# Four attention heads' logits issued together, with four PSUM banks for logits and two for everything else

## The chip, the cores and the metric

The kernel runs on one core of one Trainium2 chip. The metric is device time in microseconds (us) of that core. TensorE is PE below, its weight loads are PEld, VectorE is DVE, ScalarE is ACT and GpSimd is POOL.

## The reference, cut to what matters

The input is 4 images of 128 channels and 64x64 pixels. Everything is fp32.

```python
y  = layernorm_over_channels(x);  y = y + depthwise_3x3(y)
xw = y cut into windows of 16x16 pixels
q, k, v = xw @ Wq, Wk, Wv                   # 2 branches, 4 heads of 32
logits  = q . k over a 5x5 neighbourhood, scaled
o  = softmax(logits) . v
x  = x + (o @ Wo, the branches combined)
t  = tokens of x
t  = t + causal_linear_attention(layernorm(t))
t  = t + recurrence(batchnorm(layernorm(t) @ W))    # sigmoid(wx + y @ V.T), step by step
```

The change concerns the window attention. It is 16 bands of 16 image rows, each of four windows, and behind each band runs the causal linear attention of the band before. The recurrence at the end is the same in both kernels.

## The kernel before

The kernel takes PSUM in banks of 512 fp32 columns. Three pools share eight of them (3 + 2 + 3):

```python
ps_s = main.enter_context(tc.tile_pool(name="ps_s", bufs=3, space=PSUM))   # logits
ps_o = main.enter_context(tc.tile_pool(name="ps_o", bufs=1, space=PSUM))   # ops, dps: one bank each
ps_m = main.enter_context(tc.tile_pool(name="ps_m", bufs=3, space=PSUM))   # everything else

def bank(pool=ps_m, tag="bank"):
    return pool.tile([P, 512], F32, tag=tag, name=tag)
```

"Everything else" is q, k, v of a window, the normalisations, and all of the linear attention. A normalisation keeps one bank (`vps`) for its variances and takes a further one for each chunk:

```python
def variance(vps, at, src, n, keep=None):      # keep is given for the band's own normalisation
    cps = bank()
    nc.tensor.matmul(cps[:, : n * P], center, src, start=True, stop=True)         # L161
    if keep is not None:
        nc.vector.tensor_copy(keep, cps[:, : n * P])                               # L163
    sq = p2.tile(...)
    nc.scalar.activation(sq[:, : n * P], cps[:, : n * P], AF.Square)               # L165
    for j in range(n):
        nc.tensor.matmul(vps[:, at + j : at + j + 1], sq[:, j * P : ...], mean_col, ...)  # L167
# [...] then rstd on DVE (L156); spread() makes diag from it on POOL (L145) and multiplies on PE (L149)
```

The logits of one head use one row group of 32 rows of the PE array and get a bank of their own. The weighted sums end in a reciprocal on DVE and an addition on POOL, which only feeds a check of the final result:

```python
def logits(w, heads):
    sps = {h: bank(ps_s, "sps") for h in heads}
    # [...] mask, L266
    for br, n in pieces:
        for h in heads:
            nc.tensor.matmul(sps[h][:, cols], w["k"][rows, ...], w["q"][rows, cols], ...)  # L271
    # [...] exp on ACT, L280

def weighted(w):
    # [...] L293, L301, L304 into ops and dps
    nc.vector.reciprocal(rden, dps)                              # L306
    nc.gpsimd.tensor_tensor(rtot, rtot, rden, ALU.add)           # L307
    nc.vector.tensor_tensor(oT, ops, rden, ALU.mult)             # L309
    nc.vector.tensor_tensor(rmin, rmin, rden, ALU.min)           # L310

# the loop over windows; the framework's scheduler orders each engine's instructions from this
if now:  logits(now, (0, 1))
if done: weighted(done)              # of the window before
next(behind, None)                   # a piece of the linear attention
if now:  logits(now, (2, 3))
next(behind, None)
# [...] output of the window before, normalisation of the next band (in the second window),
#       q, k, v of the next window, two more pieces of linear attention
```

## Time and profile before

| | before |
|---|---|
| median of 2 runs | 1768.87 us (1767.15 to 1770.59) |
| span and granted clock of the profiled run | 1750.5 us, 0.886 |
| PE, DVE, ACT, POOL busy | 89%, 62%, 31%, 22% |
| one steady band, windows A, B, C, D | 16.6, 21.2, 18.0, 41.0 us |

L149 has two forms, one for the linear attention (128x512) and one for the next band's normalisation (128x384). The columns of the view of groups are: line, engine and operation, output and inputs, shapes, count; then busy us and mean ns of one; then the us that the engine stood idle just before, and for what.

```profile
L167 PE MATMUL bank<-mean_col,sq 128*128 128x1 f32 x800 | 122.9, 275 | 28.9 <-ACT sq L165 28.5
...
L244 PE MATMUL bank<-wvT,y 128*128 128x256 f32 x384 | 94.2, 382 | 0.0
L307 POOL TENSOR_TENSOR rtot<-rtot,rden 128x512 f32<-128x512 f32 x64 | 81.2, 1268 | 418.8 <-DVE rden L306 398.1 <-DVE rstd L156 20.7
L149 PE MATMUL bank<-diag,ones 128*128 128x512 f32 x128 | 76.4, 682 | 15.5 <-POOL diag L145 15.4
...
L149 PE MATMUL bank<-diag,ln_g 128*128 128x384 f32 x96 | 67.8, 852 | 33.2 <-POOL diag L145 33.2
```

PE waits 28.9 us for the normalisation's squares (L167), not at all for v (L244), and little for the diag of the linear attention (the first form of L149). The second form, before the next band, waits 33.2 us.

### The profile page before, as it was taken

The page shows a single profiled execution, that of the slowest core. Times are in us where ns is not written, and L with a number is a line of the kernel's source. Part 1 is how long each engine was busy: PE and PEld are TensorE (multiplying, and loading weights), DVE is VectorE, ACT ScalarE, POOL GpSimd, SP SyncE. Part 2 cuts the span into 40 slices and gives each one's busy share as a digit, 9 for nine tenths or more (in the row PEclk, how much of TensorE's full clock was granted, in tenths as well). Part 3 has the DMA queues.
Part 4 walks back from the last instruction along what each step waited for, and adds up shares of the span by engine and source line. Part 5 has one row for each costly group of instructions (what it writes and reads, how often), then busy time and mean ns, then how long its engine had stood idle before and what let it go on. Part 6 is the DMA issues. An engine that isn't in the chain of part 4 may idle for free. (4 is left out here: it accounts for less than half of the span.)

```text
span 1750.5 us, 27470 instructions
## 1 busy us (share of the span) xinstructions
PE 1561.3 (89%) x11294; PEld 1048.6 (60%) x11294; DVE 1083.5 (62%) x2028; ACT 540.0 (31%) x924; POOL 383.2 (22%) x683
## 2 busy tenths in 40 slices
PE   5899999899998999899998999899998999976475
PEld 3566666576666666675766666665766666644232
DVE  3666656665666766575665766575656666644298
ACT  1332323333232333332232333332232333321142
POOL 1113121311213131211212131211212131211044
PEclk8888979897889999897889999897889999887596
DMA  1000000000000000000000000000000000000422
GB/s 53 1 15 1 27 1 12 15 1 26 1 27 1 27 1 14 13 7 21 1 27 1 27 1 22 6 7 20 1 27 1 27 1 13 1 13 0 204 85 110
DMA packets 13528, 37.61 MB, mean 21 GB/s; under 512 B 3409, under 2 KB 4690, under 8 KB 12882
## 3 DMA queue, kind: packets, MB, share of 16 engines
q1 hardware_dynamic: 11664, 30.88, 5.0%
q10 hardware_dynamic: 1730, 4.89, 0.7%
q8 instruction: 91, 1.49, 0.4%
q14 instruction: 43, 0.35, 0.1%
HBM read 18.98 MB, written 16.78 MB: 20 GB/s over the span
## 5 line engine op out<-in xcount | busy, mean ns | idle before, releaser
L271 PEld LDWEIGHTS sps<-q_sb,k_sb 32*128 32x128 f32 x3072 | 260.0, 192 | 93.9 <-issue 77.3
L271 PE MATMUL sps<-q_sb,k_sb 32*128 32x96 f32 (+1 forms) x3072 | 294.0, 285 | 0.0
L306 DVE RECIPROCAL rden<-dps 128x512 f32<-128x512 f32 x64 | 214.9, 3357 | 86.0 <-PE dps L304 85.0
L225 DVE SCALAR_TENSOR_TENSOR y<-ypad,cpe_w,y 128x256 f32<-128x256 f32 x512 | 244.2, 479 | 11.0
L280 ACT ACTIVATE es<-sps 128x512 f32<-128x512 f32 x256 | 141.7, 595 | 322.5 <-PE sps L271 322.2
L145 POOL TENSOR_SCALAR diag<-ident,rstd 128x128 f32<-128x128 f32 x400 | 146.9, 387 | 417.4 <-DVE rstd L156 276.2
L307 POOL TENSOR_TENSOR rtot<-rtot,rden 128x512 f32<-128x512 f32 x64 | 81.2, 1268 | 418.8 <-DVE rden L306 398.1
L167 PEld LDWEIGHTS bank<-mean_col,sq 128*128 128x128 f32 x800 | 114.5, 220 | 72.0 <-ACT sq L165 69.4
L167 PE MATMUL bank<-mean_col,sq 128*128 128x1 f32 x800 | 122.9, 275 | 28.9 <-ACT sq L165 28.5
L304 PE MATMUL dps<-es,ones 128*32 128x512 f32 x512 | 134.5, 666 | 0.0
L238 ACT COPY k_sb<-bank 128x512 f32<-128x512 f32 x64 | 37.5, 585 | 298.0 <-PE bank L234 298.0
L165 ACT ACTIVATE sq<-bank 128x512 f32<-128x512 f32 (+1 forms) x112 | 61.7, 551 | 200.5 <-DVE xc L163 104.9
L362 POOL TENSOR_TENSOR f<-f,low 128x512 f32<-128x512 f32 x64 | 81.5, 1275 | 186.1 <-ACT low L361 185.6
L149 PE MATMUL bank<-diag,ln_g 128*128 128x384 f32 x96 | 67.8, 852 | 33.2 <-POOL diag L145 33.2
L244 PE MATMUL bank<-wvT,y 128*128 128x256 f32 x384 | 94.2, 382 | 0.0
L149 PE MATMUL bank<-diag,ones 128*128 128x512 f32 x128 | 76.4, 682 | 15.5 <-POOL diag L145 15.4
L233 PE MATMUL bank<-y,wqT 128*128 128x256 f32 x256 | 82.3, 425 | 8.3 <-DVE y L225 8.3
L293 PE MATMUL ops<-es,v_sb 128*32 128x96 f32 (+1 forms) x3072 | 87.6, 257 | 0.0
L266 PE MATMUL sps<-mask_q,mask_k 32*128 32x512 bf16 x256 | 70.4, 398 | 19.2 <-ACT es L280 12.4
L236 DVE COPY q_sb<-bank 128x512 f32<-128x512 f32 x64 | 44.2, 691 | 69.8 <-PE bank L233 69.8
L361 ACT ACTIVATE low<-low 128x512 f32<-128x512 f32 x64 | 40.3, 631 | 138.3 <-DVE low L358 138.3
L244 PEld LDWEIGHTS bank<-wvT,y 128*128 128x128 f32 x384 | 73.7, 192 | 10.3
(129 smaller groups left out, 2415.7 us busy)
## 6 DMA issues: line engine op xcount, KB each, us to landing
wxd<-wxs SPq DMA_DIRECT2D x32, 256.0 KB, 2.0
out<-ot SPq DMA_DIRECT2D x16, 512.0 KB, 2.6
x_t<-in_x SPq DMA_DIRECT2D x8, 576.0 KB, 4.0
x_t<-in_x SPq DMA_DIRECT2D x8, 544.0 KB, 4.0
wx<-wxd SPq DMA_DIRECT2D x2, 2048.0 KB, 17.5
wx<-wxd ACTq DMA_DIRECT2D x2, 2048.0 KB, 13.0
x_t<-in_x SPq DMA_DIRECT2D x8, 32.0 KB, 3.8
awT<-in_awT ACTq DMA_DIRECT2D x1, 192.0 KB, 3.5
```

The lines of the kernel that those rows point to most:

```text
L145: nc.gpsimd.tensor_scalar(diag[:, j * P : (j + 1) * P], ident, rstd[j], 1.0, ALU.mult, ALU.mult)
L149: nc.tensor.matmul(bc[:, : n * P], rows, diag[:, : n * P], start=True, stop=True)
L167: nc.tensor.matmul(vps[:, at + j : at + j + 1], sq[:, j * P : (j + 1) * P], mean_col, start=True, stop=True,)
L225: nc.vector.scalar_tensor_tensor(y2v, src, cpe_w[:, tap : tap + 1], y2v, ALU.mult, ALU.add)
L233: nc.tensor.matmul(qps[:, cols], wqT[:, br * P : (br + 1) * P], y2, start=True, stop=True)
L244: nc.tensor.matmul(vps[:, c0 : c0 + 256], y2[:, k0 : k0 + P], wvT, start=True, stop=True)
L271: nc.tensor.matmul(sps[h][:, cols], w["k"][rows, k0 : k0 + P], w["q"][rows, cols], start=False, stop=(br, n) == pieces[-1],)
L280: nc.scalar.activation(es, sps[h], AF.Exp, scale=scale)
L293: nc.tensor.matmul(ops[rows, cols], w["v"][:, n, c0 : c0 + HD], w["es"][h][:, cols], start=(br, n) == pieces[0], stop=(br, n) == pieces[-1],)
L304: nc.tensor.matmul(dps[rows], ones[:, :HD], w["es"][h], start=False, stop=True)
L306: nc.vector.reciprocal(rden, dps)
L362: nc.gpsimd.tensor_tensor(f, f, low, ALU.add)
```

## The change

The intent: four heads sit in four row groups, which can run beside each other. Two heads at a time use half of the array. Issuing all four needs four banks for logits, and the fourth is taken from "everything else".

```diff
-    ps_s = main.enter_context(tc.tile_pool(name="ps_s", bufs=3, space=PSUM))
+    ps_s = main.enter_context(tc.tile_pool(name="ps_s", bufs=4, space=PSUM))
     ps_o = main.enter_context(tc.tile_pool(name="ps_o", bufs=1, space=PSUM))
-    ps_m = main.enter_context(tc.tile_pool(name="ps_m", bufs=3, space=PSUM))
+    ps_m = main.enter_context(tc.tile_pool(name="ps_m", bufs=2, space=PSUM))
@@
         if now:
-            logits(now, (0, 1))
+            logits(now, (0, 1, 2, 3))
         if done:
             weighted(done)
         next(behind, None)
-        if now:
-            logits(now, (2, 3))
         next(behind, None)
```

## The prediction

> **What bounds the kernel now.** I began with busy shares on the profile page, then cut one steady band of image rows (16 such bands make the attention stage) into its four windows, and then read the instruction timeline inside them.
>
> ```profile
> PE 1561.3 (89%) x11294; PEld 1048.6 (60%) x11294; DVE 1083.5 (62%) x2028; ACT 540.0 (31%) x924; POOL 383.2 (22%) x683
> ...
> L271 PE MATMUL sps<-q_sb,k_sb 32*128 32x96 f32 (+1 forms) x3072 | 294.0, 285 | 0.0
> L306 DVE RECIPROCAL rden<-dps 128x512 f32<-128x512 f32 x64 | 214.9, 3357 | 86.0 <-PE dps L304 85.0
> ```
>
> TensorE (PE) leads with 89%, VectorE (DVE) has 62%, and the logits (L271) are PE's largest group. The stretches, one window each, are: time, then busy us per engine, then the granted PE clock.
>
> ```profile
> core 0: us, PE busy (x) PEld busy (x) DVE busy (x) ACT busy (x) POOL busy (x), PEclk, DMA share, GB/s
> 451.25:467.86 16.61, 16.61 (x110) 13.13 (x109) 12.05 (x34) 6.14 (x10) 3.95 (x10) 1.00 0.01 1
> 467.86:489.03 21.17, 21.00 (x193) 15.38 (x191) 14.33 (x34) 6.34 (x11) 2.56 (x3) 1.00 0.01 2
> 489.03:507.07 18.04, 16.67 (x138) 9.79 (x138) 12.66 (x18) 6.56 (x12) 4.39 (x9) 0.95 0.08 30
> 507.07:548.10 41.03, 36.47 (x260) 24.03 (x259) 22.59 (x32) 12.62 (x20) 11.18 (x21) 0.83 0.06 15
> ```
>
> I call them A, B, C, D; together 96.85 us. In A and B PE has no idle time, so PE issue sets the pace. In D PE sits idle 4.6 us although all its other work is done: that is the next band's normalisation, where one chain of single instructions runs alone:
>
> ```profile
> 534.66 0.81 PE L161 MATMUL bank<-x_t,center 128*128 128x384 f32 x2
> ...
> 536.08 0.55 DVE L163 COPY xc<-bank 128x384 f32<-128x384 f32 x1
> ...
> 536.72 0.49 ACT L165 ACTIVATE sq<-bank 128x384 f32<-128x384 f32 x1 [3.03 <-DVE xc L163]
> ...
> 537.26 0.83 PE L167 MATMUL bank<-mean_col,sq 128*128 128x1 f32 x6 [1.47 <-ACT sq L165]
> ...
> 537.95 1.54 PE L161 MATMUL bank<-x_t,center 128*128 128x384 f32 x4
> 538.88 1.20 DVE L163 COPY xc<-bank 128x384 f32<-128x384 f32 x2 [1.06 <-PE bank L161]
> ```
>
> The last L161 row holds two of the three chunks at once (x4: two fp32 passes each): chunks two and three use two banks at the same time. Last, what a head's logits cost alone and beside another head:
>
> ```profile
> 105.20 1.58 PE L271 MATMUL sps<-q_sb,k_sb 32*128 32x96 f32 x24
> ...
> 126.87 1.57 PE L271 MATMUL sps<-q_sb,k_sb 32*128 32x96 f32 x12
> ```
>
> The first row is 24 passes of two heads that alternate, the second 12 passes of one head alone, both at full clock: the same time. So the row groups run beside each other, and a stretch of logits costs what its longest row group costs: in the second the single passes start 0.112 us apart on the mean of the trace's records, so a matmul of two passes costs 0.224 us.
>
> **What the Trainium skill says.** "TensorE: Matmul & The Clock Gate", Part 3 (packing small matmuls), says that matmuls in different row groups overlap, and gives 3.07x for four row tiles. The rows above show 2x for two; no row of this kernel has four heads at once, though L293 keeps four column tiles going (48 passes in about 1.09 us). "TensorEngine Tiling (Array Packing)", Gotcha 1, says that row tiling raises PSUM pressure because row tiles need different banks: that is the trade made here. "PSUM — Partial Sum Buffer", on bank collisions, has two engines' accesses to one bank put in order; in the trace L165 on ScalarE (ACT) waits for L163 on DVE each time (48 waits, 104.9 us), though both only read. The clock-gate page's Part 1 ties the clock to PE activity; here D, with its idle PE, has 0.83 granted and A and B have 1.00.
>
> **The change part by part**, per band; I compared the built order of each engine before and after.
>
> *Logits.* Cut the order into uninterrupted runs of L271 and take from each the count of its longest row group. Before, a band has 19 runs with 61 matmuls in the longest groups: 61 x 0.224 = 13.7 us. The L271 time in such a run not covered by the matmul before it sums to 257 us over the trace, 16.1 a band, so each run costs (16.1 - 13.7) / 19 = 0.12 us beside. After: 21 runs, 31 matmuls, 6.9 + 2.6 = 9.5 us. Gain 6.5 us, if four groups scale as two do.
>
> *Causal-attention loops* (L405, L409, L411, in A and B). With three banks the next numerator starts while the last is being read. With two, L405 waits for DVE's state add and L411 for the yt multiply; the built order shows both waits. A step on DVE is rd 0.16, state 0.28, reciprocal 0.16, yt 0.34 with one or two tap multiplies of 0.47 between. Laid beside 0.65 us of matmuls and shorter logits, I get some 0.2 us idle at each of six steps: loss 1.2 us.
>
> *Normalisation* (D). The running variance holds one bank, so two banks leave one for the chunks: L161, copy, square, L167, three times in a row. A chunk takes about 0.65 + 0.55 + 0.6 + 0.55 = 2.4 us; the two that ran together before took 0.8 less than two such chains, and the built order puts nothing between: loss 1.5 us. Also, DVE's order after has the second softmax reciprocal (3.36 us) just before the first L163. Before, that reciprocal came earlier, and L163 started 0.6 us after L161 ended. Adding 3.36 us behind the aT multiply, the residual add and the multiplies gives 3 us from L161's end to the copy: loss 2.4 us.
>
> *Window C.* The weighted sums now sit in a clump, so the reciprocal of one runs when C's q copy and the rstd reciprocal want DVE, and the rtot add (1.27 us) now stands before the four diag instructions (1.41 us) on POOL. PE's L149 then starts about 6.4 us after the first L233, against 492.54 - 489.03 = 3.5 before; some 1 us of that is work of its own, so loss 2.3 us. In D the L149 before the linear attention has no logits left to hide its diag behind: loss 1.1 us.
>
> Sum: 6.5 - 1.2 - 3.9 - 2.3 - 1.1 = -2.0 us a band. With 15 bands behind the first, that is 30 us lost, or 1799 us. I take 1796, a little less, because the last band has no next normalisation to wait for.
>
> **The rivals.** (1) PE is the bound, and the whole logits gain lands: 16 x 6.5 = 104 us, 1665 us. For it: PE 89%. Against: the built order shows the waits above on exactly the banks that were taken away. (2) Half of it lands, because the losses in C and D hide behind weighted sums that I placed wrongly: 1768.87 - 50 = 1720 us. (3) Four row groups don't scale, with a quarter more per pass: 9.5 becomes some 11.2 us, another 27 us lost, 1825 us. (4) The longer idle time of PE in D draws a lower clock into C and A; window D already pays about 4 us for half-clock stretches, and as much again in each band would be 64 us, 1850 us.
>
> **Range and chances.** The net is a difference of 6.5 and 8.5, each good to perhaps 2 us, so about 3 us a band, 48 us: 1745 to 1850. Under 1733 everything in C and D would have to be free: 0.12. Over 1804 needs 0.3 us a band more than I have: 0.36. The rest, 0.52, is within 2%.
>
> **What would show it.** L271's rows should hold four heads, with its busy time down by a third or so. PE's idle time before L405 or L411 should be there for DVE, where the page of before has 4.1 us for L405. L167's wait for sq (28.5 us of PE idle time) should at least double. The normalisation from the first L161 to the first L233, 13.4 us before, should be near 17. If L405 doesn't wait and that stays at 13 us, the banks weren't needed and I am wrong towards faster; if A to D all grow with the clock down, towards slower.

## More of the kernel before

The timeline of POOL around window C of the prediction shows why the first form waits so little. The addition L307 has run long before rstd comes, and diag starts at once:

```profile
484.10 1.27 POOL L307 TENSOR_TENSOR rtot<-rtot,rden 128x512 f32<-128x512 f32 x1 [5.20 <-DVE rden L306]
491.08 3.12 POOL L145 TENSOR_SCALAR diag<-ident,rstd 128x128 f32<-128x128 f32 x8 [5.71 <-DVE rstd L156]
```

## The result, and the profile after

The changed kernel took 1885.37 us (1884.81 to 1885.93, two runs). The ratio to before is 1.066, with a 95% interval of 1.061 to 1.071. Ratios here are the mean time of one kernel's runs over that of the other's in the same rounds, so not quite the ratio of the quoted medians. Executions over 1.5% slower than the fastest of the same kernel are left out of the means. The prediction was 1796 us with a range to 1850: right that the change doesn't pay, wrong on how much it costs.

The page of the changed kernel, the lines for the engines, the logits and the softmax reciprocal:

```profile
PE 1564.7 (83%) x11294; PEld 936.6 (50%) x11294; DVE 1083.7 (58%) x2028; ACT 537.5 (29%) x924; POOL 385.1 (20%) x683
...
L306 DVE RECIPROCAL rden<-dps 128x512 f32<-128x512 f32 x64 | 214.6, 3353 | 35.4 <-PE dps L304 35.3
...
L271 PE MATMUL sps<-q_sb,k_sb 32*128 32x96 f32 (+1 forms) x3072 | 195.7, 304 | 0.0
```

The logits' busy time fell from 294.0 to 195.7 us, yet PE's total rose by 3 us. So nearly as much was added in other matmuls, which are the same in number: they ran slower, or with less beside them (busy times of lines that run beside each other overlap, so this is no exact balance). The span and the mean granted clock of the two profiled runs, before and then after:

```profile
core 0: 1750.5 us, clock 0.886
```
```profile
core 0: 1882.7 us, clock 0.862
```

One band of the changed kernel in its four windows A to D, cut at the same instruction as in the prediction (the first L233 of each window); columns as there:

```profile
core 0: us, PE busy (x) PEld busy (x) DVE busy (x) ACT busy (x) POOL busy (x), PEclk, DMA share, GB/s
697.73:716.94 19.21, 19.11 (x142) 12.62 (x141) 12.55 (x34) 6.16 (x10) 4.46 (x9) 0.97 0.01 1
716.94:740.38 23.44, 22.51 (x217) 14.77 (x215) 14.38 (x33) 6.95 (x12) 1.53 (x3) 1.00 0.01 1
740.38:755.52 15.14, 11.24 (x78) 6.06 (x76) 12.13 (x19) 3.64 (x6) 4.53 (x9) 1.00 0.05 18
755.52:803.17 47.65, 38.57 (x264) 22.09 (x265) 22.47 (x31) 14.75 (x25) 11.20 (x21) 0.76 0.06 19
```

D grew by 6.6 us, and its clock fell from 0.83 to 0.76. A and B grew by 2.6 and 2.3 us, and C shrank by 2.9, but some matmuls only changed places: C has 78 left of 138. The mean over the steady bands is about 98 us before (single bands take 93 to 104) and 106.6 after. I then charged every moment of PE's timeline of these bands to the matmul that kept PE until then, or to the wait before it:

| us a band | before | after |
|---|---|---|
| logits L271 | 16.4 | 10.9 |
| the causal loops L405, L409, L411 | 6.9 | 7.9 |
| L161, L167, L149 (normalisations and spreads) | 22.1 | 26.2 |
| PE idle, all | 5.7 | 13.6 |
| of it before L167 / L149 / L301 / L244 | 1.8 / 2.3 / 0.2 / 0.0 | 4.0 / 4.5 / 1.9 / 1.1 |

The groups that answer to the five of before:

```profile
L167 PE MATMUL bank<-mean_col,sq 128*128 128x1 f32 x800 | 134.0, 287 | 64.8 <-ACT sq L165 64.3
...
L244 PE MATMUL bank<-wvT,y 128*128 128x256 f32 x384 | 106.4, 406 | 17.0 <-ACT k_sb L238 10.2 <-ACT v_sb L248 5.8 <-DVE q_sb L236 0.9
L149 PE MATMUL bank<-diag,ones 128*128 128x512 f32 x128 | 95.6, 839 | 42.6 <-POOL diag L145 42.6
...
L149 PE MATMUL bank<-diag,ln_g 128*128 128x384 f32 x96 | 71.2, 887 | 30.9 <-POOL diag L145 30.9
L307 POOL TENSOR_TENSOR rtot<-rtot,rden 128x512 f32<-128x512 f32 x64 | 81.3, 1271 | 404.9 <-DVE rden L306 259.9 <-DVE rstd L156 139.2 <-DVE xc L163 5.9
```

Three waits have grown or appeared. L167 and the first form of L149 wait more than twice as long; the second form waits about as long as before. L244 now waits for the copies of k and v, whose banks it needs. And L307 is now often released at the moment when rstd arrives: 139.2 us, against 20.7 before. That is the sign of an addition that stands just ahead of diag.

The logits in the timeline, four heads at once, 16 and 32 passes (a head has 4 and 8 of them; a pass is one record of the trace, and an fp32 matmul has two):

```profile
645.56 0.70 PE L271 MATMUL sps<-q_sb,k_sb 32*128 32x96 f32 x16
...
659.32 1.15 PE L271 MATMUL sps<-q_sb,k_sb 32*128 32x64 f32 x32
```

The normalisation at the end of D, in the timeline. The number in brackets is how long the engine stood idle before, and for what:

```profile
677.30 0.91 PE L161 MATMUL bank<-x_t,center 128*128 128x384 f32 x2
677.35 3.35 DVE L306 RECIPROCAL rden<-dps 128x512 f32<-128x512 f32 x1
680.61 0.49 DVE L163 COPY xc<-bank 128x384 f32<-128x384 f32 x1
...
681.74 1.44 PE L167 MATMUL bank<-mean_col,sq 128*128 128x1 f32 x6 [0.61 <-ACT sq L165]
...
683.04 1.63 PE L161 MATMUL bank<-x_t,center 128*128 128x384 f32 x2
...
685.90 1.44 PE L167 MATMUL bank<-mean_col,sq 128*128 128x1 f32 x6 [1.23 <-ACT sq L165]
...
687.20 1.63 PE L161 MATMUL bank<-x_t,center 128*128 128x384 f32 x2
```

The first copy L163 waits behind the 3.35 us reciprocal. Then the chunks go strictly one after the other, 4.16 us apart (683.04 to 687.20), because one bank is left for them. And the same L161 that took 0.91 us takes 1.63 from the second chunk on: the clock records of the trace have full clock until 681.68 and half of it until 698.75. Summed over twelve steady bands, the time at half clock is 27.3 us a band here, against 18 to 20 before, as one chooses the twelve. L161 takes 1.8 times as long there (1.63 for 0.91 us), so I estimate that these 7 to 9 us can be up to some 4 us of loss a band.

The start of C, where the linear attention needs its rstd:

```profile
740.51 3.36 DVE L306 RECIPROCAL rden<-dps 128x512 f32<-128x512 f32 x1 [1.03 <-PE dps L304]
...
743.10 1.13 PE L244 MATMUL bank<-wvT,y 128*128 128x256 f32 x4 [0.73 <-ACT k_sb L238]
743.78 0.14 DVE L156 RECIPROCAL rstd<-std 128x8 f32<-128x8 f32 x1
...
744.01 1.27 POOL L307 TENSOR_TENSOR rtot<-rtot,rden 128x512 f32<-128x512 f32 x1 [8.87 <-DVE rstd L156]
...
745.25 3.28 POOL L145 TENSOR_SCALAR diag<-ident,rstd 128x128 f32<-128x128 f32 x8
...
747.19 1.12 PE L149 MATMUL bank<-diag,ones 128*128 128x512 f32 x2 [1.53 <-POOL diag L145]
```

The softmax reciprocal holds up rstd, then the addition holds up diag by 1.24 us, and PE waits 1.53 us for it. (The addition needs only rden, the reciprocal's result; that ends 0.05 us before rstd, so the view names rstd, the later of the two.) L149 starts 6.8 us after the first L233, where it was 3.5.

### The profile page after: what moved, and what is told of

It is laid out like the page before. It is cut to its first block, busy times and chain, and to the rows that moved or that the text cites. A ratio compares the mean times of both kernels' runs of the same rounds, so it can differ in the third digit from the quotient of the medians.

```text
span 1882.7 us, 27496 instructions
## 1 busy us (share of the span) xinstructions
PE 1564.7 (83%) x11294; PEld 936.6 (50%) x11294; DVE 1083.7 (58%) x2028; ACT 537.5 (29%) x924; POOL 385.1 (20%) x683
## 5 line engine op out<-in xcount | busy, mean ns | idle before, releaser
L271 PEld LDWEIGHTS sps<-q_sb,k_sb 32*128 32x128 f32 x3072 | 143.8, 196 | 105.3 <-issue 83.2
L271 PE MATMUL sps<-q_sb,k_sb 32*128 32x96 f32 (+1 forms) x3072 | 195.7, 304 | 0.0
L280 ACT ACTIVATE es<-sps 128x512 f32<-128x512 f32 x256 | 138.0, 601 | 194.0 <-PE sps L271 193.7
L167 PE MATMUL bank<-mean_col,sq 128*128 128x1 f32 x800 | 134.0, 287 | 64.8 <-ACT sq L165 64.3
L167 PEld LDWEIGHTS bank<-mean_col,sq 128*128 128x128 f32 x800 | 124.4, 235 | 123.9 <-ACT sq L165 122.8
L307 POOL TENSOR_TENSOR rtot<-rtot,rden 128x512 f32<-128x512 f32 x64 | 81.3, 1271 | 404.9 <-DVE rden L306 259.9
L149 PE MATMUL bank<-diag,ones 128*128 128x512 f32 x128 | 95.6, 839 | 42.6 <-POOL diag L145 42.6
L244 PE MATMUL bank<-wvT,y 128*128 128x256 f32 x384 | 106.4, 406 | 17.0 <-ACT k_sb L238 10.2
L293 PE MATMUL ops<-es,v_sb 128*32 128x96 f32 (+1 forms) x3072 | 109.8, 259 | 0.0
L293 PEld LDWEIGHTS ops<-es,v_sb 128*32 128x32 f32 x3072 | 74.1, 118 | 64.6 <-issue 52.6
L304 PE MATMUL dps<-es,ones 128*32 128x512 f32 x512 | 105.4, 601 | 0.0
L149 PE MATMUL bank<-diag,ln_g 128*128 128x384 f32 x96 | 71.2, 887 | 30.9 <-POOL diag L145 30.9
L358 DVE TENSOR_SCALAR low<-bank,ab 128x512 f32<-128x512 f32 x64 | 47.7, 746 | 81.6 <-PE bank L356 81.6
L233 PE MATMUL bank<-y,wqT 128*128 128x256 f32 x256 | 80.8, 433 | 15.6 <-DVE y L225 8.3
L244 PEld LDWEIGHTS bank<-wvT,y 128*128 128x128 f32 x384 | 65.6, 190 | 51.5 <-ACT k_sb L238 19.8
L356 PE MATMUL bank<-xl,awTc 128*128 128x512 f32 x128 | 84.1, 792 | 1.6 <-DVE xl L351 1.6
## 6 DMA issues: line engine op xcount, KB each, us to landing
wx<-wxd SPq DMA_DIRECT2D x2, 2048.0 KB, 17.7
```

What stands on the lines that cost most here:

```text
L149: nc.tensor.matmul(bc[:, : n * P], rows, diag[:, : n * P], start=True, stop=True)
L244: nc.tensor.matmul(vps[:, c0 : c0 + 256], y2[:, k0 : k0 + P], wvT, start=True, stop=True)
L271: nc.tensor.matmul(sps[h][:, cols], w["k"][rows, k0 : k0 + P], w["q"][rows, cols], start=False, stop=(br, n) == pieces[-1],)
L280: nc.scalar.activation(es, sps[h], AF.Exp, scale=scale)
L293: nc.tensor.matmul(ops[rows, cols], w["v"][:, n, c0 : c0 + HD], w["es"][h][:, cols], start=(br, n) == pieces[0], stop=(br, n) == pieces[-1],)
L304: nc.tensor.matmul(dps[rows], ones[:, :HD], w["es"][h], start=False, stop=True)
```

## The experiments

The theory after this reading: (1) the third bank for everything else is the main loss, through the normalisation's chunks; (2) four heads at once do shorten the logits, but they bunch the weighted sums, and these stand on DVE and POOL in front of what PE needs next. Rivals: the order of the heads is what costs, not the banks; the clock costs by itself; four row groups don't scale.

| run | banks logits/else | heads | chunks of the band's normalisation in | ratio (95% interval) |
|---|---|---|---|---|
| the change | 4/2 | four | else | 1.066 (1.061 to 1.071) |
| e1 | 4/2 | pairs | else | 1.061 (1.056 to 1.066) |
| e2 | 3/2 | pairs | else | 1.073 (1.067 to 1.080) |
| e3 | 3/3 | three, one | else | 1.037 (1.033 to 1.041) |
| e4 | 4/2 | four | logits | 1.021 (1.016 to 1.026) |
| e7 | 4/2 | four, filler matmuls | else | 1.060 (1.055 to 1.065) |
| e8 | 4/2 | pairs | logits | 1.012 (1.009 to 1.014) |
| e9 | 3/3 | pairs | logits | 0.990 (0.983 to 0.997) |
| e6 | 6 shared | four | shared | 1.008 (1.006 to 1.011) |
| e6b | 6 shared | pairs | shared | 1.064 (1.059 to 1.069) |
| e10 | 4/2 | four, q copy on ACT | logits | 1.033 (1.027 to 1.040) |
| e11 | 4/2 | four, no addition L307 | logits | 0.982 (0.978 to 0.987) |
| e12 | 3/3 | pairs, no addition | else | 1.005 (0.997 to 1.012) |
| e13 | 3/3 | pairs, no addition | logits | 0.999 (0.993 to 1.005) |
| e15 | 4/2 | four, no addition | else | 1.050 (1.046 to 1.055) |
| e14 | 4/2 | four, addition on DVE | logits | 0.992 (0.987 to 0.997) |
| e16 | 4/2 | four, sum on ACT | logits | 0.983 (0.976 to 0.989) |
| e17 | 4/2 | as e14, v in logits banks too | logits | 1.006 (0.999 to 1.012) |

All outputs are right. Each ratio is against the kernel before in the same rounds. The kernel before itself ran at medians of 1751.5 to 1769.5 us in the different rounds, so I compare ratios between rounds and not times; a "point" below is 0.01 of the ratio, some 17.7 us or 1.1 us a band.

### Banks or order: e1, e2, e3

e1 changes the banks and keeps the pairs:

```diff
-ps_s ... bufs=3        +ps_s ... bufs=4
-ps_m ... bufs=3        +ps_m ... bufs=2
```

> The kernel before with the changed banks (four for logits, two for the rest) and its own issue order, two heads and two heads. If the lost third bank is the cause and issuing four heads together pays for itself, this must be slower than the changed kernel by the logits time that the change saved, 5.5 us a band or some 89 us: about 1970 us, 1.11 of before. If it is the clump of four heads (weighted sums and softmax reciprocals bunched) that costs, this stays within 2% of before, about 1780 us.

Measured: 1864.38 us, 1.061, which neither expectation had (1.11 or within 2%). The banks alone cost 6.1 of the 6.6 points; the intervals of e1 and of the change overlap. In e1 the logits take 13.7 us a band (16.4 before, 10.9 with four heads), PE's idle time before L167 grows by 2.7 us, and the clock is 0.859. So a shorter time for the logits, 2.8 us a band, came with the order of the heads, and nothing of it arrived in the total.

e2 takes the third bank away and gives the logits no fourth:

```diff
-ps_m ... bufs=3        +ps_m ... bufs=2        # ps_s stays at 3
```

> The kernel before with two banks for everything else instead of three, and three (not four) for logits: seven of eight banks used, heads in pairs. If the lost third bank is all of the cost and the fourth logits bank is worth nothing while heads go in pairs, this equals the run with four and two banks in pairs: 1864 us, ratio 1.055 to 1.067. Rival: the fourth logits bank already paid (there L271 took 2.7 us a band less than before); without it 16 x 2.7 = 43 us more, ratio about 1.085. The normalisation from the first L161 to the first L233 should be near 17.2 us, as there, in both.

Measured: 1891.22 us, 1.073: between the two expectations, 1.2 points over e1. So the fourth logits bank is worth something even to pairs. The waits of PE that lead are the normalisation's: 69.0 us of idle time before L167 for the square, 64 times. That is the one wait which grew by more than 0.6 us a band (1.8 to 4.4).

e3 keeps the banks of before and issues three heads, then one:

```diff
-logits(now, (0, 1))        +logits(now, (0, 1, 2))
-logits(now, (2, 3))        +logits(now, (3,))
```

> The kernel before with its own three and three banks, and heads issued three together and then one. If issue width helps where no bank is lost, the logits take less than the 16.4 us of a band of before, some 13 us, and no wait is added: about 1725 us, 0.975 of before. If wider issue itself brings the loss by bunching what follows it, the time is 1780 us or more.

Measured: 1818.53 us, 1.037. The logits shrink by 2.1 us a band and PE's idle time grows by 2.9, of it 1.7 before the transposes L386 that wait for POOL. All three banks are there, so the order of the heads can lose time without any bank taken away. It is another order than the change's, though, so it says nothing on how much the order costs there.

### The chunks of the normalisation: e4, e8, e9

These take the chunks of a band's normalisation from the logits pool:

```diff
-        cps = bank()
+        cps = bank() if keep is None else bank(ps_s, "sps")
```

e4 is the changed kernel with this edit, e8 is e1 with it, and e9 is the kernel before with it.

> The changed kernel, with the three chunks of the next band's normalisation written to the logits' four banks instead of the two others. If the single bank left for the chunks is the main cost (20.4 us from the first chunk to the next window's projections, against 13.4 before), that stretch falls to 13 us or less and some 100 us come back: about 1785 us, 1.01 of before. If the loss lies in the other windows, this stays above 1850 us.

> The kernel before with four and two banks, heads in pairs, and the normalisation's chunks in the logits' banks. With the changed kernel (1.066), the banks alone (1.061) and the four heads with chunks moved (1.021) this fills a square of two by two. If four heads at once pay nothing, because what they save turns into waits, this lands where the four heads did, 1.015 to 1.025. If the four heads' saving lands once the normalisation is unblocked, this is some 50 us slower than those, 1.05 or more.

> The kernel before, three and three banks and pairs, only with the normalisation's chunks in the logits' banks. If the chunks wait for banks even with three, their chain (14.2 us of TensorE time almost alone) hides beside other work and the time falls to about 1715 us, 0.98. If three banks were enough there, it stays within 1% of before.

Measured: e4 1789.11 us, 1.021; e8 1777.2 us, 1.012; e9 1738.49 us, 0.990. The one line gives back 4.5 points to four heads and 5.0 to pairs, and only 1.0 where there are three banks. So the lost bank acts through these chunks above all, and in the same way in either order of the heads. In e4 PE's idle time before L167 is 0.9 us a band against 4.0; most chunks lie 0.65 to 1.6 us apart in the steady bands. The waits before L244 and L233, the other users of the two banks, stay as they were (1.1 and 0.5 us a band), so what came back isn't theirs. With the chunks moved, four heads are still 0.9 points behind pairs: the second loss is to be looked for there.

### The clock: e7

e7 is the changed kernel with three matmuls of no use for each chunk, which keep PE busy while it waits. They write columns of `vps` that nobody reads, so the result stays right.

```diff
+        if keep is not None:
+            for _ in range(3):
+                nc.tensor.matmul(vps[:, 128:512], center, src, start=True, stop=True)
         sq = p2.tile([P, 512], F32, tag="sq", name="sq")
```

> The changed kernel with three matmuls of no use (128x384) after each chunk's centring matmul in the normalisation, into columns of the variance bank that nobody reads, so TensorE stays busy while it waits. If the half clock that TensorE gets in its idle time stretches the chain (4.16 us a chunk in the trace, against some 2.5 at full clock), a chunk falls to about 2.7 us and the kernel gains 4 us a band, about 1820 us. If the clock is only an onlooker, the fillers add nothing or cost up to 1 us a chunk: 1885 to 1930 us.

Measured: 1856.34 us (1841 to 1864), 1.060 with an interval that overlaps the change's, and between the two expectations. The mean clock rose from 0.862 to 0.914 in the profiled run, the fastest of the four (the others have 0.896 to 0.903), and the time at half clock fell from 27.3 to between 12 and 13 us a band. PE's timeline of e7 in the normalisation (L166 is the filler, L170 is what was L167):

```profile
679.45 0.89 PE L161 MATMUL bank<-x_t,center 128*128 128x384 f32 x2
680.18 2.10 PE L166 MATMUL bank<-x_t,center 128*128 128x384 f32 x6
682.12 0.72 PE L170 MATMUL bank<-mean_col,sq 128*128 128x1 f32 x6
682.70 0.89 PE L161 MATMUL bank<-x_t,center 128*128 128x384 f32 x2
```

At full clock L161 takes 0.89 us instead of 1.63, and L167 0.72 instead of 1.44: 1.46 us less for a chunk. Although the filler adds 2.10 us, which is longer than the wait that it fills, a chunk takes 3.25 us in place of 4.16, and D is 2.9 us shorter in the profiled run (47.6 to 44.7 on the mean). So half clock is a good part of why the serial chain is so long. That it makes much of the total time isn't shown: the timed ratio moved by 0.6 points, within the intervals.

### One pool for both: e6 and e6b

One pool of six banks in place of two, with four heads (e6) and with pairs (e6b):

```diff
-ps_s ... bufs=4 ; ps_m ... bufs=2
+ps_s ... bufs=6 ; bank(pool=ps_s, tag="sps")
```

> Four heads at once, with one pool of six banks for the logits and all the rest, in place of four and two. If it is the split that starves the rest, this gains what moving the chunks gained and more, since the causal loops get third banks too: 1.00 of before or less. If the logits of the next window take the banks early and hold them, it stays at 1.05.

> The kernel before, heads in pairs, with one pool of six banks for logits and everything else. Four heads at once in the same pool gave 1.008. If four heads at once cost 0.5 to 0.9 per cent by themselves (as in the two pairs of runs with the bank split fixed), this is 0.999 to 1.003 of the time before. Rival: four heads at once lose only because banks are fixed, and with a shared pool they pay: then this is slower than 1.008.

Measured: e6 1771.56 us, 1.008; e6b 1872.94 us, 1.064. My expectation for e6b (0.999 to 1.003) was a plain miss, and so was the rival's. In both, PE waits 6.5 us a band before L301 for the softmax's banks (0.2 in the kernel before), so a shared pool brings an order of its own. In e6b window D takes 52.5 us. I didn't find out why pairs suffer so much more from it; that stays open. e6 shows all the same that the order with four heads need not cost 6 points once no work is confined to two banks.

### POOL's addition: e10, e11, e12, e13, e15

e10 was a first try at the second loss: e4, with the q copy moved from DVE to ACT and the addition L307 issued later in the program.

```diff
-        nc.vector.tensor_copy(q_sb, qps)                      +        nc.scalar.copy(q_sb, qps)
-        nc.gpsimd.tensor_tensor(rtot, rtot, rden, ALU.add)    # moved to the output of the window
```

> Four heads with the chunks in the logits' banks, and with two things taken off what window C waits for: the q copy from VectorE to ScalarE, and the rtot add issued later, so it doesn't stand before the diag instructions. If the bunched reciprocals block C through these two (2.4 us of idle TensorE time a band more than before, in front of L149 and L244), this falls by some 30 us from the four heads with chunks moved, to 1.00 of before or less. If the wait only passes on to the rstd reciprocal behind the same softmax reciprocal, it stays at 1.015 or more.

Measured: 1819.8 us, 1.033, slower than e4. In POOL's timeline two of a band's four additions still end where a diag begins, as in e4, so the order that the edit meant to change had stayed. So the run says nothing on the additions. With the q copy on ACT, PE's wait before L244 did fall from 1.1 to 0.3 us a band; but the time at half clock rose from 20 to 25 us a band, and the whole was slower. Which of the two edits did that isn't shown.

e11 is e4 without the addition. The check that it feeds is weaker then; the outputs are the same.

```diff
-        nc.gpsimd.tensor_tensor(rtot, rtot, rden, ALU.add)
```

> Four heads at once, the chunks of the normalisation in the logits banks (1789 us, 1.021), and without the addition into rtot on POOL (the flag that it feeds is then weaker, the outputs stay right). If the additions, bunched in front of the diag instructions on POOL, are why L149 waits 2.3 us a band longer there than in the kernel before, L149's idle time falls by some 1.5 to 2 us a band and the time by 24 to 32 us: ratio 1.003 to 1.008. Rival: L149 waits for DVE (rstd behind a 3.35 us softmax reciprocal) and the freed POOL changes nothing: ratio 1.018 to 1.024.

Measured: 1725.84 us, 0.982: 3.9 points less than e4, twice what I had expected, and faster than the kernel before. POOL's timeline in the normalisation, first of e4:

```profile
644.89 1.26 POOL L307 TENSOR_TENSOR rtot<-rtot,rden 128x512 f32<-128x512 f32 x1 [7.59 <-DVE rstd L156]
646.13 2.54 POOL L145 TENSOR_SCALAR diag<-ident,rstd 128x128 f32<-128x128 f32 x6
```

and of e11:

```profile
619.35 2.61 POOL L145 TENSOR_SCALAR diag<-ident,rstd 128x128 f32<-128x128 f32 x6 [11.05 <-DVE rstd L156]
```

In e4 POOL has been idle for 7.59 us, and at the moment when rstd arrives it does the addition first, whose own input, held up by the same reciprocal, came 0.07 us earlier. In e11 it starts diag. The waits of PE, in the view of groups, are 38.7 and 38.2 us in e4 and 22.1 and 22.5 in e11:

```profile
L149 PE MATMUL bank<-diag,ones 128*128 128x512 f32 x128 | 91.8, 808 | 38.7 <-POOL diag L145 38.7
...
L149 PE MATMUL bank<-diag,ln_g 128*128 128x384 f32 x96 | 69.6, 872 | 38.2 <-POOL diag L145 38.2
```
```profile
L149 PE MATMUL bank<-diag,ones 128*128 128x512 f32 x128 | 85.0, 752 | 22.1 <-POOL diag L145 22.1
...
L149 PE MATMUL bank<-diag,ln_g 128*128 128x384 f32 x96 | 71.0, 888 | 22.5 <-POOL diag L145 22.5
```

Together that is 32 us of some 69 (0.039 x 1769). Over the steady bands, the idle time before L149 falls from 4.6 to 2.1 us. I haven't traced the rest to one wait. The time at half clock is down from some 20 to 15 us a band, which I estimate at up to 2.5 us a band, enough to be the rest; and C, which took 15.1 to 17.7 us, takes 13.9 in nearly all bands.

Is it the addition as such, or its place? e12 takes it out of the kernel before, e13 out of e9, and e15 out of the changed kernel, by the same one line.

> The kernel before without the addition into rtot on POOL (its flag is weaker then, the outputs stay right). If only the bunching by four heads at once puts the additions on the path, pairs gain little: 0.99 to 1.00. Rival: POOL's additions cost each order as much as they cost the four heads with the chunks in logits banks (63 us of 1789): ratio 0.96 to 0.97.

> Pairs, three and three banks, the normalisation's chunks in logits banks (0.990 with the addition), without the addition into rtot. Bunching alone: 0.98 to 0.99, so no better than four heads without the addition (0.982). Rival: 0.95 to 0.96, and pairs stay ahead of four heads by the 3 per cent by which they led with the addition (1.021 against 0.990).

> The changed kernel (1.066) without the addition into rtot, the chunks still in the two banks for everything else. If the addition costs the four heads the same wherever the chunks are, 1.03 (63 us less). If the lost bank hides it (the chunk chain waits for DVE in any case), above 1.045. The wait of L167 for sq should stay near 4 us a band in both; the wait of L149 should fall from 4.5 to about 2 us a band.

Measured: e12 1776.8 us, 1.005; e13 1762.08 us, 0.999; e15 1854.86 us, 1.050. Pairs gain nothing (e13's interval overlaps e9's, and e13 missed its 0.98 to 0.99). Four heads gain 3.9 points with the chunks moved and 1.6 points without. The place shows in POOL's timelines: counted over twelve steady bands, the additions that end just where a diag begins are none a band in the kernel before, e1, e2 and e3, one in e8, e9 and the changed kernel, and two in e4. So four heads at once put one there, and moving the chunks puts one there too, even with pairs. That its removal is worth nothing to pairs is less clear than the ratios look: from e9 to e13 PE's idle time before L149 fell from 2.5 to 1.5 us a band, but the time at half clock rose from 16 to 24 us. Why the clock was lower isn't known, and pairs with four and two banks were not run without the addition. In e15 the wait of L149 fell too, and the wait of L167 stayed:

```profile
L167 PE MATMUL bank<-mean_col,sq 128*128 128x1 f32 x800 | 134.7, 287 | 64.4 <-ACT sq L165 64.0
...
L149 PE MATMUL bank<-diag,ones 128*128 128x512 f32 x128 | 86.2, 762 | 23.4 <-POOL diag L145 23.4
```

So the two losses are separate waits, and the first hides part of the second.

### Versions that keep the whole check: e14, e16, e17

e14 is e4 with the addition on DVE, behind the minimum. e16 is e4 with the sum of each window's reciprocals taken on ACT into a column of its own:

```diff
-        nc.gpsimd.tensor_tensor(rtot, rtot, rden, ALU.add)
         nc.vector.tensor_tensor(rmin, rmin, rden, ALU.min)
+        nc.vector.tensor_tensor(rtot, rtot, rden, ALU.add)                              # e14
+        nc.scalar.activation(junk, rden, AF.Copy, accum_out=rtot[:, n : n + 1])         # e16
```

> Four heads at once, chunks in logits banks, the addition into rtot kept but on DVE, behind the minimum (64 times about 0.7 us of DVE). If POOL's order in front of diag is what cost, DVE has room (58 per cent busy) and most of the gain stays: ratio 0.985 to 1.000, faster than the kernel before with the whole check kept. Rival: the addition is as much in the way on DVE, in front of q_sb, rstd and xc: 1.01 to 1.02.

> Four heads at once, chunks in logits banks, and the sum of the reciprocals taken on ACT (a copy with an accumulated sum, one column a window) in place of the addition on POOL; the check stays whole. On DVE this was 0.992, without any 0.982. ACT is 29 per cent busy; if the place matters only by what waits behind it, 0.983 to 0.990. Rival: 64 more ACT instructions of some 0.6 us stand in front of the exponentials and copies that PE waits for: 0.995 to 1.01.

Measured: e14 1752.0 us, 0.992; e16 1729.32 us, 0.983. e16 is the best version that keeps the check whole, and it beats both kernels. Its page shows where the room was: ACT 34% and POOL 18% busy, PE 50 us less than in either kernel.

```profile
PE 1512.1 (88%) x11294; PEld 911.8 (53%) x11294; DVE 1066.3 (62%) x2029; ACT 581.3 (34%) x1052; POOL 310.2 (18%) x619
```

e17 is e14 with the two v banks of a window taken from the logits pool as well:

```diff
-                vps = bank()            # in window_inputs
+                vps = bank(ps_s, "sps")
```

> As the run with the addition on DVE (0.992), with the two v banks of each window's inputs taken from the logits banks too. If the 1.1 us a band that PE waits before L244 is a bank wait (v's bank is q's until the q copy has read it), it vanishes, and the time falls by 1.1 x 16 = 18 us: 0.980 to 0.985. Rival: it waits for y or for its own operands, and stays: 0.99 to 0.995; or v then waits for the exponentials to free a logits bank: 1.00 or more.

Measured: 1772.13 us, 1.006, slower than e14. The group of v in e17:

```profile
L244 PE MATMUL sps<-wvT,y 128*128 128x256 f32 x384 | 109.2, 397 | 11.2 <-ACT es L280 10.5 <-ACT v_sb L248 0.7
```

The wait before L244 for the copy of k is gone, and a wait for an exponential (L280) to free a logits bank stands in its place. So it was a bank wait, and moving it to the other pool doesn't buy it off. Two banks for q, k and v cost about 1.1 us a band with four heads. Only e10 took most of it away (0.3 left), and e10 was slower.

## Why the prediction was right or wrong

The waits that it named came, beside two that it left out (L244 and L233), so the mechanism was right in the main; what failed is the size of the terms. The sum at the end of this part shows by how much. Four heads at once (the logits' gain less the causal loops) were to bring 5.3 us a band and brought 2.0. The normalisation on one bank was to cost 3.9 and cost 5.0. The addition was to cost 3.4 and cost 4.3.

**The logits' gain (6.5 us a band): right in kind, a little too large.** L271 fell from 16.4 to 10.9 us, 5.5. Four row groups did scale as two do, as it had assumed. A row of the timeline counts its last pass with its full length (0.27 us), so short rows seem dear. From start to start, where all heads of a run step together at full clock, passes of 96 columns follow each other after 0.112 us in the median and 0.133 on the mean with four heads (114 steps), and after 0.112 and 0.132 with two heads before (468 steps). So its third rival, a quarter more per pass, is not what happened. Where four heads have got out of step, a step takes 0.158 us on the mean (93 steps); that is part of the missing 1.0 us, and the rest I haven't separated.

**The causal loops (1.2 us): right in size, not in kind.** It expected idle time of PE at each of six steps. They took 1.0 us more, but as time charged to the matmuls; the idle time before L405 grew by only 0.2. Why the matmuls took longer isn't shown, so the agreement is in part luck.

**The normalisation (1.5 + 2.4 = 3.9 us): the wait that was mis-sized most clearly, in its first term.** On the mean over fifteen bands, the stretch from the first L161 to the next first L233 grew from 14.2 to 19.7 us. The first chunk, behind the reciprocal, cost about what was predicted: 5.2 us to the second chunk instead of 3.3, so 1.9 (5.6, so 2.3, in the median band). But from the second chunk to the third it was 4.0 instead of 1.0 us, so 3.0 and not 1.5. The 1.5 doesn't follow from its own lines either: they give 0.8 for the chains, and the other 0.7 has no working. "A chunk takes about 0.65 + 0.55 + 0.6 + 0.55 = 2.4 us" used the full-clock times of the trace before. The serial chain ran at half clock, which alone is 1.46 us a chunk by e7. The fourth rival had this, for D as a whole, but its 1850 us doesn't follow from its 64 us: on top of the 1799 of the sum they make 1863.

**Windows C and D, L149 behind the addition (2.3 + 1.1 = 3.4 us): right in mechanism, too large beside the lost bank and too small without it.** L149 starts 6.8 us after the first L233, for which the prediction has 6.4. In the changed kernel PE's idle time before L149 grew by 2.2 us a band, all of it in the form for the linear attention (0.2 to 2.5; the other form fell from 2.1 to 1.9), and removing the addition gave 1.6 points, 1.7 us a band. Removing it from e4 gave 3.9 points, 4.3 us a band.

**What the prediction left out.** A and B were taken as unchanged but for the causal loops. PE now waits 1.1 us a band before L244 and 0.5 before L233, and part of D's and C's matmuls moved into A and B, so windows compared one by one mislead.

**The sum (-2.0 us a band).** Measured it is 0.066 x 1769 / 16 = -7.3. The runs cut it in three. The chunks in two banks: (1.066 - 1.021) x 1769 / 16 = 5.0, for which it had 3.9. The addition: (1.021 - 0.982) x 1769 / 16 = 4.3, for 3.4. With both relieved, four heads are 0.018 x 1769 / 16 = 2.0 us faster, for which it had 6.5 - 1.2 = 5.3. Each is good to 0.5 to 0.8 us, by the intervals, and they depend on the order in which one takes them (e15). So in this order all three terms were on the wrong side: 1.1, 0.9 and 3.3 us, together 5.3. Of the last, the logits' smaller gain is 1.3 (L271 takes 11.2 us in e11) and the waits before L244 and L233 are 1.7.

**The checks that it named.** L167's wait more than doubled (28.9 to 64.8 us), as said. L405's grew from 4.1 to 9.1 us, partly for DVE's state. The normalisation was to be near 17 us and was near 20, and "A to D all grow with the clock down, towards slower" is close to what was seen, except for C.

## What to carry to other kernels

A bank was priced here by the chain of single steps that it let overlap, not by the engine that it feeds; before giving one up, look for the stretch where everything else waits on one such chain. When such a chain becomes serial, price it also at the half clock that such a PE got here, not only at the one in the present profile. And issuing work in bunches moves its tail on the other engines too: a 1.27 us instruction that nobody waits for held up diag by 1.24 us when it came to stand in front of it.

## What the Trainium skill lacked or had wrong

- "TensorE: Matmul & The Clock Gate", the section on HAM oscillation, gives as its rule that PE idle gaps be no longer than some 3.4 us. Here the clock halved at 681.68 though no gap in the 30 us before was longer than 1.7 us, and it stayed half for 17 us with gaps of 0.6 to 1.9 us. So the rule alone would have passed this chain over three engines. The page's next section, on a second failure mode, does tell of clock losses from frequent short gaps, but gives no length for them. That the clock is only ever half or full, as Part 1 has it, agrees: every record in the steady bands is 0.5 or 1.0.
- The same page's Part 3 gives 3.07x for four row tiles at 512 columns. It has no figure for narrow fp32 matmuls. Here passes of 96 columns follow each other after 0.112 us in the median with four row groups as with two, so twice the groups gave twice the passes. Whole runs gain less: 24 passes in two row groups took 1.58 us, and in four row groups 16 took 0.70 and 32 took 1.15, which is 15.2 passes a us against 22.9 and 27.8.
- No page says what a bank is worth that one use gives up to another. Here the one that was taken from other work cost 6.1 points (e1), of which 5.0 came back when one user of the pool was moved (e8).
- "GPSIMD Engine Reference", section 4.1 (engine selection), advises DVE for elementwise work since GpSimd is about 2x slower on two inputs. The durations agree: 1.27 us on POOL, 0.69 on DVE (e14). But the speed didn't decide: taking it off POOL gained pairs nothing and four heads 3.9 points. The page has nothing on the place in an engine's order.
